# Adapter loads tied to batch 2, the first mask and weight blocks in quarters, and late outputs in halves, in a masked-weight and LoRA kernel

## The chip, the cores and the metric

The kernel runs on one core of a Trainium2 chip. The metric is the device time of one execution in microseconds (us), median over runs. A core has a matrix engine (PE; its weight loads are listed as PEld), a vector engine (DVE), an activation engine (ACT), a GpSimd engine (POOL) and a queue engine (SP) that here only issues transfers. Every engine runs its own instruction stream in order; semaphores make an instruction wait for another engine or for a transfer.

## The reference, cut to what matters

```python
x = x + L0(x, W0, b0, coeff, mask)      # x: 8 x 256 x 1024, mask: 8 x 1024 x 1024 of 0 and 1
x = x + L1(x, itok, W1, b1, lora_A, lora_B)

def L0(h, W, b, coeff, mask):
    sign = 2 * mask - 1                               # +1 or -1
    return einsum('bsi,oi->bso', h, W) + b + einsum('bsi,bio->bso', h, sign) * coeff[:, None, None]

def L1(x, mapping, W, b, lora_As, lora_Bs):           # 32 adapters of rank 16
    h = einsum('bti,bir->btr', x, lora_As[mapping])
    return einsum('bti,oi->bto', x, W) + b + einsum('btr,bro->bto', h, lora_Bs[mapping]) * 2.0
```

All numbers are float32. The mask is 4 MB for each of the eight batches, so that 32 MB of mask have to be read beside 4 MB for each of the two weights and 8 MB of `x`.

## The kernel before, in words

**First layer.** For batch b the effective weight is W0 + I + coeff(b) * (2 mask - 1): `convert` (L401, ACT) turns a loaded block of mask into the signed term in place, and `add` (L314, DVE) adds the block of W0. `w0_sb` stays in SBUF for the whole kernel and the identity (the residual) is added to its diagonal. Batch 0 is multiplied densely (L486): for each of eight chunks c of 128 input rows a mask block `w_0_c` and a W0 chunk are loaded, the first four chunks (`BY_HALF`) in two halves i of the output columns. The tokens `x0_p` come with them, the first one in two halves, on ACT's and SP's queue. Batches 1 to 7 use one level of Strassen-Winograd (`seven`): blocks `w_b_i_g`, sums of blocks s1 to s4 on DVE, sums of tokens t1 to t4 on DVE, and seven products (L657) into PSUM banks X, Y, Z, V. In batch 1 the bank Z first takes s1*t1, ACT reads it out with the bias (`biased`, L569), and the product of s4 is then added to the same bank.

**Second layer.** For each group of four batches, a two-level Winograd product (`product`, L852) with W1. The sums of W1 are computed once in group 0 and kept in DRAM (`keep`, POOL's queue); group 1 loads them again (`left_again`, SP's queue). The adapters are added by `down` (L892, needs all of `la`) and `up` (L923, needs all of `lb`). `lb_pad` holds for each of the four batches 16 rows of lora_B, one row of b1 and zeros; it is cleared by a memset on POOL (L453). `adapters_begin` loads the four rows of b1, `adapters` four pairs of lora_A and lora_B rows at the slot that `itok` names (L809, L812), all on POOL's queue.

**Order.** All work is first recorded as tasks in `Plan`, each with an engine, a duration, reads and writes, and perhaps a due time or `ahead` (it is not planned earlier than so many us ahead of its latest start). `Plan.order` then places the tasks by a list scheduler with fixed costs (`RATE`, `LATENCY`, eight transfers in flight for each kind of queue), and the instructions are emitted in that order. PE's own order is the order of recording. A transfer counts on one of eight semaphores (counters 0 to 7 of SP and ACT together, in turn), so a ninth transfer waits until the one eight places ahead of it has landed. At the end of the program SP waits for these eight counters one after another, 0 first and 7 last.

**Places that the change touches.** The load loop of batch 0 (L421 to L435); the memset of `lb_pad` (L449 to L457); `due` of the two first outputs of batch 0 on DVE (L515); `adapters_begin` and `adapters`; `store`, `Run.done` and the stores of the block c22 (L1134) in the second layer; the call site (L1146); the two cost constants of `Plan`. In group 1 the last product is cut in pieces (`finish`, L1018) whose results are stored on SP, ACT and SP.

Of the kernel before, what the change touches and what calls it, by code (L numbers as in the profile page):

```python
# [13 lines left out]
P = 128  # L14
OH = 512
CG = 2
# [29 lines left out]
class Task:  # L46
    __slots__ = (
        "engine", "n", "busy", "tail", "emit", "before", "after", "bufs", "due", "ls", "ahead",
        "open", "ready", "done", "bytes", "end",
    )  # L50


class Plan:
# [4 lines left out]


    WAKE = 0.07  # L60
    RATE = 400e3
    LATENCY = {"SP": 1.5, "ACT": 1.5, "POOL": 2.5}
    LANES = 8
    MARGIN = 0.3
    TIGHT = 1.0
# [7 lines left out]
    def task(self, engine, busy, tail, emit, reads=(), writes=(), due=None, ahead=None, nbytes=0):  # L73
        k = Task()
        k.engine, k.busy, k.tail, k.emit, k.due, k.ahead = engine, busy, tail, emit, due, ahead
        k.n, k.bytes = len(self.tasks), nbytes
        k.before, k.after = {}, []
        for r in reads:
            for key in r.keys:
                self.need(k, self.writer.get((r.buf, key)))  # L80
        for r in writes:
            for key in r.keys:
                self.need(k, self.writer.get((r.buf, key)))
                for other in self.readers.get((r.buf, key), ()):
                    self.need(k, other)
        for r in reads:
            for key in r.keys:
                self.readers.setdefault((r.buf, key), []).append(k)
        for r in writes:
            for key in r.keys:  # L90
                self.writer[r.buf, key] = k
                self.readers[r.buf, key] = []
        k.bufs = list(dict.fromkeys(r.buf for r in [*writes, *reads]))
        for b in k.bufs:
            b.left += 1
        k.open = len(k.before)
        k.ready = 0.0
        k.done = False
        if engine == "PE":
            k.due = self.pe  # L100
            self.pe += busy
        self.tasks.append(k)
        return k
# [10 lines left out]
    def order(self, slots, idle):  # L114
        for k in reversed(self.tasks):
            late = [a.ls - self.WAKE - self.span(k) for a in k.after]
            if k.engine == "PE":
                late.append(k.due)
            elif k.due is not None:
                late.append(k.due - self.span(k))  # L120
            k.ls = min(late, default=self.pe)
        free = {e: 0.9 for e in ("PE", "DVE", "ACT", "POOL", "SP")}
        places = {kind: [[0.0, i, False] for i in range(n)] for kind, n in slots.items()}
        lanes = {"HW": [0.0] * self.LANES, "SW": [0.0] * self.LANES}
# [110 lines left out]
def kernel(  # L235
# [85 lines left out]
    def dma(engine, o, x, nbytes, due=None, ahead=None, what=None):  # L321
        busy = {"SP": 0.37, "ACT": 0.36, "POOL": 0.53}[engine]
        reads = [x] if isinstance(x, Ref) else []
        writes = [o] if isinstance(o, Ref) else []

        def emit():
            ENGINE[engine].dma_start(  # L327
                o.ap() if isinstance(o, Ref) else o, x.ap() if isinstance(x, Ref) else x
            )

        return plan.task(
            engine, busy, plan.LATENCY[engine], emit, reads, writes, due, ahead, nbytes
        )
# [43 lines left out]
    def x0_ref(p, c=None):  # L377
        return x0[p](ALL if c is None else (c,), (lambda t: t) if c is None else (lambda t: t[:, c]))
# [4 lines left out]
    def part(a, i):  # L383
        flat = a.rearrange("p i f -> (p i f)")
        return flat.rearrange("(i p f) -> i p f", i=2, p=P)[i]
# [25 lines left out]
    def w_part(c, i, o):  # L411
        keys = tuple((i2, q) for i2 in (ALL if i is None else (i,)) for q in halves(o))
        sel = slice(0, 2) if i is None else slice(i, i + 1)
        return w_b0[c](keys, lambda t: t[:, sel, o])
# [5 lines left out]

    every = slice(0, OH)  # L421
    for c in range(NC):
        where = [0, 1] if c < BY_HALF else [None]
        for i in where:
            n = P * OH * 4 * (1 if i is not None else 2)
            w = w_part(c, i, every)
            as_int = w.buf(w.keys, lambda t, f=w.index: f(t).bitcast(I32))
            src = lambda a: part(a, i) if i is not None else a
            sel = lambda r: r if i is None else r.buf(r.keys, lambda t, f=r.index: f(t)[:, 0])
            dma("SP", sel(as_int), src(mask[0, c]), n)  # L430
            dma("SP", sel(w0_part(c, i, every)), src(w0T[c]), n)
            if c == 0:
                dma("ACT" if i == 0 else "SP", x0_ref(0, i), part(x0T[0], i), n // 2)
            elif c % CG == 0 and i in (0, None):
                dma("SP", x0_ref(c // CG), x0T[c // CG], P * CG * T * 4)  # L435

    plan.task(
# [8 lines left out]

    ident_keys = ((0,),)
    plan.task("POOL", 1.2, 0.1, lambda: make_identity(nc, ident.t), (), (ident((0,)),), due=6.0)
    plan.task(  # L449
        "POOL",  # L450
        1.2,
        0.1,
        lambda: nc.gpsimd.memset(lb_pad.t, 0.0),  # L453
        (),
        (lb_pad(tuple(range(2 * GB))),),
        due=30.0,
    )  # L457

    def identity(c):
        h, q = divmod(c * P, OH)  # L460
# [46 lines left out]
    for ot in range(NC):  # L507
        h, j = divmod(ot, TPH)
        ps = dense[ot // 2]((0,), lambda t, k=ot % 2: t[:, k, :])
        o = y[0, h](ALL, lambda t, j=j: t[:, j, :])  # L510
        bias = b0_sb((0,), lambda t, ot=ot: t[:, ot : ot + 1])
        if ot < 2:
            xr = x0_ref(ot // CG, ot % CG)
            dve(
                lambda o=o, ps=ps, bias=bias, xr=xr: nc.vector.scalar_tensor_tensor(  # L515
                    o.ap(), ps.ap(), bias.ap(), xr.ap(), ALU.add, ALU.add
                ),
                T,
                (ps, bias, xr),
                (o,),  # L520
                due=42.0,
            )
        else:
            plan.task(
                "ACT",
                T / 1200 + 0.145,
                0.11,
                lambda o=o, ps=ps, bias=bias: nc.scalar.activation(
                    o.ap(), ps.ap(), AF.Identity, bias=bias.ap()
                ),  # L530
                (ps, bias),
                (o,),
                due=42.0,
            )
# [257 lines left out]
        for u in range(2):  # L792
            add(q[u](ALL), quads[x][u](ALL), quads[z][u](ALL), 1024, op)

    def adapters_begin():
        for i in range(GB):
            row = i * S + R
            dma("POOL", lb_pad((i,), lambda t, r=row: t[r : r + 1, :]), b1, 4096, due=60.0, ahead=25.0)

    def adapters(group):  # L800
        for i in range(GB):
# [20 lines left out]
    def second_layer(group):  # L822
# [53 lines left out]
        def store(o, i, j, u, v, q=None, c=slice(0, CG), tokens=slice(0, T), due=12.0):  # L876
# [6 lines left out]
                due=plan.pe + due,  # L883
            )

        def down():
            ph = bank(f"psh_{group}", 2, T, partial=True)

            def emit():
                for c in range(NC):  # L890
                    for i in range(GB):
                        nc.tensor.matmul(  # L892
                            ph.t[i * S : i * S + R, 0, :],
                            lhsT=la.t[:, i, c, :],
                            rhs=y[GB * group + i, c // TPH].t[:, c % TPH, :],
                            start=c == 0,
                            stop=c == NC - 1,
                        )

            reads = [la((i,)) for i in range(GB)]  # L900
            reads += [y[GB * group + i, h](ALL) for i in range(GB) for h in range(2)]
            pe(32, 3.62, emit, reads, (ph((0,)),))
            for i in range(GB):
                rows = slice(i * S, i * S + R)
                plan.task(
                    "ACT",
                    0.3,
                    0.11,
                    lambda rows=rows: nc.scalar.mul(h_sb.t[rows, :], ph.t[rows, 0, :], SCALING),
                    (ph((0,)),),  # L910
                    (h_sb((i,)),),
                )
# [38 lines left out]
        class Run:  # L951
# [10 lines left out]

            def done(self, *uv):
                if self.dest:
                    store(self.out[uv], *self.dest, *uv)
                if self.then:
                    self.then(uv)

# [161 lines left out]
        for u in range(2):  # L1130
            o2, x2 = (q[u, 0].buf(ALL) for q in (c22, e1))
            add(o2, o2, x2, 1024, due=plan.pe + 5.0)
            for v in range(2):
                store(c22[u, v], 1, 1, u, v)  # L1134
        k.x2()
        k.y()
        k.x3()
# [5 lines left out]

    for group in range(NGROUP):
        for b in range(GB * group, GB * (group + 1)):
            if b == GB * group + 2:  # L1146
                if group == 0:
                    adapters_begin()
                adapters(group)
            if b == 0:  # L1150
                continue
            if b in DENSE:
                dense_batch(b)
            else:
                seven(b)
        second_layer(group)
# [80 lines left out]
```

## Time and profile before

| | |
|---|---|
| median of 3 runs | 402.17 us (402.03 to 403.28) |
| profiled execution: its own time | 401.81 us |
| its span, first to last instruction | 400.1 us |
| PE busy | 394.5 us, 2750 matmuls |
| PEld busy | 360.9 us |
| DVE busy | 326.0 us, 409 instructions |
| ACT busy | 143.3 us |
| POOL busy | 44.4 us |
| moved by transfers | 84.63 MB, mean 211 GB/s |

The span is the time between the first and the last recorded instruction on the core; 1.7 us of the execution's own time lie outside of it. A group's row in the profile gives the line, the engine, the operation, the tile names without numbers, the shape, the busy time and the idle time of the engine ahead of it with what ended that. Big buffers (128 x 1024) all have the name `big`, half ones `small`, PSUM banks `bank`: which product a row is follows from its line and its place in the order.

### The profile page before, as it was taken

What the parts mean: (1) busy time and instruction counts of PE and PEld (TensorE: products, weight loads), DVE (VectorE), ACT (ScalarE), POOL (GpSimd) and SP (SyncE); (2) the same over time, 40 slices, a digit from 0 to 9 for tenths busy, and PEclk for the clock granted to TensorE, in tenths of its full rate; (3) what the DMA queues carried; (4) which work ended last, traced back from release to release, by engine and by line L of the source; (5) the groups of instructions that cost most, each with busy time, mean ns of one, the idle gap of its engine ahead of it and who ended that gap; (6) DMA issues with size and microseconds to landing.
All of it is one profiled execution on the core that took longest, in us unless ns stands there. A gap on an engine that the chain in (4) does not pass through costs nothing.

```text
span 400.1 us, 6933 instructions
## 1 busy us (share of the span) xinstructions
PE 394.5 (99%) x2750; PEld 360.9 (90%) x2750; DVE 326.0 (81%) x409; ACT 143.3 (36%) x249; POOL 44.4 (11%) x87
## 2 busy tenths in 40 slices
PE   8999999999999999999999999999999999999996
PEld 6889999999978888888899999999998888888885
DVE  3548999999999999997999999999737356485574
ACT  5438974712133021017318266472222231100200
POOL 3000400001344241230223000000000000000000
DMA  8999999641477389579679665110101457555934
GB/s 275 400 404 410 367 365 408 218 153 40 172 242 284 113 280 360 196 246 326 242 238 321 207 207 207 61 54 2 26 2 54 114 154 241 177 157 176 290 112 159
DMA packets 30676, 84.63 MB, mean 211 GB/s; under 512 B 4276, under 2 KB 4916, under 8 KB 30644
## 3 DMA queue, kind: packets, MB, share of 16 engines
q1 hardware_dynamic: 24914, 67.19, 49.1%
q0 software_dynamic: 5440, 16.80, 11.2%
q8 instruction: 22, 0.36, 0.4%
q10 hardware_dynamic: 290, 0.20, 0.2%
q14 instruction: 10, 0.08, 0.1%
HBM read 64.25 MB, written 19.92 MB: 210 GB/s over the span
## 4 chain that ended last, share of the span: by engine, by line
PE 83%; DMA 12%; DVE 2%; issue 1%; ACT 1%; SPq 1%
PE bank L852 40%; PE bank L657 39%; DMA big<-mask 9%; DMA w<-w0T 3%; DVE big L314 2%; PE bank L923 2%; PE bank L892 2%; SPq L327 1%; PE bank L1018 0%; ACT big L401 0%; ACT big L569 0%
## 5 line engine op out<-in xcount | busy, mean ns | idle before, releaser
L314 DVE TENSOR_TENSOR big<-big,big 128x1024 f32<-128x1024 f32 (+1 forms) x104 | 116.7, 1138 | 6.7 <-PE bank L657 4.3
L657 PE MATMUL bank<-small,big 128*128 128x128 f32 x896 | 103.6, 275 | 0.3 <-DVE big L314 0.3
L657 PEld LDWEIGHTS bank<-small,big 128*128 128x128 f32 x896 | 101.8, 192 | 0.5 <-DVE big L314 0.5
L314 DVE TENSOR_TENSOR big<-bank,big 128x512 f32<-128x512 f32 (+2 forms) x103 | 68.5, 677 | 38.7 <-PE bank L852 32.1
L852 PE MATMUL bank<-small,small 128*128 128x256 f32 x384 | 89.1, 380 | 0.1
L401 ACT ACTIVATE big<-big,neg_c,two_c 128x1024 f32<-128x1024 int32 (+2 forms) x69 | 79.3, 1182 | 18.7 <-DMA big<-mask 18.3
L314 DVE TENSOR_TENSOR big<-big,w 128x1024 f32<-128x1024 f32 (+2 forms) x69 | 76.8, 1142 | 9.6 <-DMA w<-w0T 5.5
L852 PEld LDWEIGHTS bank<-small,small 128*128 128x128 f32 x384 | 72.7, 190 | 11.1 <-issue 0.8
L657 PE MATMUL bank<-big,big 128*128 128x128 f32 x672 | 78.4, 275 | 0.8 <-ACT big L569 0.8
L657 PEld LDWEIGHTS bank<-big,big 128*128 128x128 f32 x672 | 76.8, 192 | 1.1 <-ACT big L569 1.0
L569 ACT ACTIVATE big<-bank,b 128x128 f32<-128x128 f32 x112 | 32.3, 367 | 73.0 <-PE bank L657 63.5
L852 PE MATMUL bank<-big,small 128*128 128x256 f32 x224 | 52.5, 380 | 0.0
L852 PEld LDWEIGHTS bank<-big,small 128*128 128x128 f32 x224 | 42.3, 190 | 6.3 <-ACT big L318 0.7
L318 ACT COPY bank<-bank 128x512 f32<-128x512 f32 x20 | 11.4, 570 | 85.7 <-PE bank L852 61.8
L318 ACT COPY big<-bank 128x512 f32<-128x512 f32 x32 | 17.6, 593 | 56.7 <-PE bank L852 30.6
L314 DVE TENSOR_TENSOR small<-big,small 128x512 f32<-128x512 f32 x49 | 33.2, 685 | 2.6 <-PE bank L852 2.5
L486 PE MATMUL bank<-small,big 128*128 128x256 f32 x128 | 29.1, 387 | 0.1
L486 PEld LDWEIGHTS bank<-small,big 128*128 128x128 f32 x128 | 24.4, 193 | 4.7 <-DVE big L314 1.0
L852 PE MATMUL bank<-big,big 128*128 128x256 f32 x112 | 26.7, 381 | 0.0
L852 PEld LDWEIGHTS bank<-big,big 128*128 128x128 f32 x112 | 21.0, 190 | 3.4 <-ACT big L318 0.7
L314 DVE TENSOR_TENSOR small<-big,big 128x512 f32<-128x512 f32 x28 | 19.2, 685 | 2.3 <-PE bank L852 2.1
L314 DVE TENSOR_TENSOR small<-big 128x512 f32<-128x512 f32 x28 | 19.2, 684 | 2.1 <-PE bank L852 2.1
(38 smaller groups left out, 122.0 us busy)
## 6 DMA issues: line engine op xcount, KB each, us to landing
big<-mask SPq DMA_DIRECT2D x60, 512.0 KB, 7.2
big<-xT SPq DMA_DIRECT2D x14, 512.0 KB, 5.3
big<-w1T SPq DMA_DIRECT2D x8, 512.0 KB, 4.9
leaf_S_s<-small POOLq DMA_DIRECT2D x16, 256.0 KB, 3.8
outT<-big POOLq DMA_DIRECT2D x16, 256.0 KB, 2.8
small<-leaf_S_s SPq DMA_DIRECT2D x16, 256.0 KB, 3.2
outT<-big SPq DMA_DIRECT2D x15, 256.0 KB, 2.5
leaf_A_s<-small POOLq DMA_DIRECT2D x12, 256.0 KB, 3.0
```

Of the source, the lines that this page charges most:

```text
L314: return dve(lambda: f(o.ap(), x.ap(), y.ap()), n, (x, y), (o,), due)
L318: "ACT", n / 1200 + 0.06, 0.11, lambda: nc.scalar.copy(o.ap(), x.ap()), (x,), (o,), due
L327: ENGINE[engine].dma_start(o.ap() if isinstance(o, Ref) else o, x.ap() if isinstance(x, Ref) else x)
L401: lambda: nc.scalar.activation(o.ap(), x.ap(), AF.Identity, bias=neg_c.t[:, b : b + 1], scale=two_c.t[:, b : b + 1]),
L486: nc.tensor.matmul(dense[ot // 2].t[:, ot % 2, :], lhsT=w_b0[c].t[:, h, j * P : (j + 1) * P], rhs=x0[c // CG].t[:, c % CG, :], start=c == ...
L569: lambda o=o, p=p, bias=bias: nc.scalar.activation(o.ap(), p.ap(), AF.Identity, bias=bias.ap()),
L657: nc.tensor.matmul(ps[:, j, :], lhsT=l[:, c, j * P : (j + 1) * P], rhs=m[:, 2 * a + c, :], start=first and a == 0 and c == 0 and j == 0, s ...
L852: nc.tensor.matmul(ps.t[:, j, :], lhsT=lt[:, c, j * P : (j + 1) * P], rhs=rt[:, c, :], start=start and c == 0 and j == 0, stop=False, skip ...
L892: nc.tensor.matmul(ph.t[i * S : i * S + R, 0, :], lhsT=la.t[:, i, c, :], rhs=y[GB * group + i, c // TPH].t[:, c % TPH, :], start=c == 0, s ...
L923: nc.tensor.matmul(ps[b].t[:, j, :], lhsT=lb_pad.t[rows, o : o + P], rhs=h_sb.t[rows, :], start=j == 0, stop=j == 1, skip_group_check=True,)
```

## The change

The loads of batch 0's first chunk are issued in two quarters and one half (mask and W0 in turn) in place of two halves, and are given the first rank in the planner (`rank`). The memset of `lb_pad` is moved from the start of the program into `adapters_begin`, behind a small ACT copy that reads an element column of batch 2's `y`; a second such copy stands ahead of `la`. `adapters_begin` and `adapters` are recorded one batch later (after batch 2). The rows of b1 lose their due time. The first outputs of batch 0 get the due time 65 in place of 42. Five stores of group 1 (four of c22, one of the last but one block) are issued as two transfers each. `RATE` and `LATENCY` of the planner are changed a little, which moves the order of some other tasks.

```diff
@@ class Plan
-    RATE = 400e3
-    LATENCY = {"SP": 1.5, "ACT": 1.5, "POOL": 2.5}
+    RATE = 396e3
+    LATENCY = {"SP": 1.8, "ACT": 1.8, "POOL": 2.8}
...
-            k.ls = min(late, default=self.pe)
+            k.ls = min(late, default=self.pe) if k.rank is None else k.rank
@@ the loads of batch 0
     for c in range(NC):
-        where = [0, 1] if c < BY_HALF else [None]
-        for i in where:
-            n = P * OH * 4 * (1 if i is not None else 2)
-            w = w_part(c, i, every)
+        where = [(0, every), (1, every)] if c < BY_HALF else [(None, every)]
+        for i, o in parts(0) if c == 0 else where:
+            n = P * (o.stop - o.start) * 4 * (1 if i is not None else 2)
+            w = w_part(c, i, o)
...
-            dma("SP", sel(as_int), src(mask[0, c]), n)
-            dma("SP", sel(w0_part(c, i, every)), src(w0T[c]), n)
-            if c == 0:
-                dma("ACT" if i == 0 else "SP", x0_ref(0, i), part(x0T[0], i), n // 2)
+            for r, a in ((sel(as_int), mask[0, c]), (sel(w0_part(c, i, o)), w0T[c])):
+                dma("SP", r, src(a), n).rank = -1.0 if c == 0 else None
+            if c == 0 and o.stop == OH:
+                dma("ACT" if i == 0 else "SP", x0_ref(0, i), part(x0T[0], i), P * T * 4)
...
-    plan.task(
-        "POOL",
-        1.2,
-        0.1,
-        lambda: nc.gpsimd.memset(lb_pad.t, 0.0),
-        (),
-        (lb_pad(tuple(range(2 * GB))),),
-        due=30.0,
-    )
...
-                due=42.0,
+                due=65.0,
@@ the adapters
-    def adapters_begin():
+    def behind(o, late):
+        plan.task(
+            "ACT",
+            0.2,
+            0.11,
+            lambda: nc.scalar.copy(o.ap(), late.ap().to_broadcast(list(o.ap().shape))),
+            (late,),
+            (o,),
+        )
+
+    def adapters_begin(late):
+        rows = lb_pad(tuple(range(2 * GB)), lambda t: t[:, :1])
+        behind(rows, late)
+        behind(la(tuple(range(GB)), lambda t: t[:, :, 0, 0]), late)
+        plan.task("POOL", 1.0, 0.1, lambda: nc.gpsimd.memset(lb_pad.t, 0.0), (), (rows,))
         for i in range(GB):
             row = i * S + R
-            dma("POOL", lb_pad((i,), lambda t, r=row: t[r : r + 1, :]), b1, 4096, due=60.0, ahead=25.0)
+            dma("POOL", lb_pad((i,), lambda t, r=row: t[r : r + 1, :]), b1, 4096, ahead=25.0)
@@ the second layer
+        def store_halves(o, *where):
+            for half in [slice(c, c + 1) for c in range(CG)] if tail else [slice(0, CG)]:
+                store(o.buf(o.keys, lambda t, f=o.index, h=half: f(t)[:, h]), *where, c=half)
...
-                    store(self.out[uv], *self.dest, *uv)
+                    whole = self.n + 1 < len(OUTER) or uv != (0, 0)
+                    (store if whole else store_halves)(self.out[uv], *self.dest, *uv)
...
-                store(c22[u, v], 1, 1, u, v)
+                store_halves(c22[u, v], 1, 1, u, v)
@@ the call site
-            if b == GB * group + 2:
+            if b == GB * group + 3:
                 if group == 0:
-                    adapters_begin()
+                    adapters_begin(y[2, 0]((0,), lambda t: t[:, 0, :1]))
                 adapters(group)
```

## The prediction

> **What bounds the kernel now.** I read four views in turn: the page's shares and its chain, PE's waits, windows of the stretches with transfers, and the timeline around each wait of PE. First the page's shares, then PE's waits (line, released by: us in total, times, longest):
>
> ```profile
> PE 394.5 (99%) x2750; PEld 360.9 (90%) x2750; DVE 326.0 (81%) x409; ACT 143.3 (36%) x249; POOL 44.4 (11%) x87
> PE bank L348 <- PEq L1226: 0.9, 1, 0.9
> PE bank L657 <- ACT big L569: 0.8, 1, 0.8
> PE bank L657 <- DVE big L314: 0.3, 1, 0.3
> ```
>
> PE is the bound: apart from its start and two waits in batch 1 it hardly pauses. The change adds and removes no matmul, so it can gain only at PE's start, at these two waits and behind PE's end, and lose wherever it makes a new wait. The timeline around both waits (start, length, [idle before <- releaser]):
>
> ```profile
> 45.97 8.04 DVE L314 TENSOR_TENSOR big<-big,big 128x1024 f32<-128x1024 f32 x7
> 47.25 5.62 PE L657 MATMUL bank<-small,big 128*128 128x128 f32 x48 [0.34 <-DVE big L314]
> 48.61 1.12 ACT L569 ACTIVATE big<-bank,b 128x128 f32<-128x128 f32 x4
> 51.36 1.24 ACT L401 ACTIVATE big<-big,neg_c,two_c 128x1024 f32<-128x1024 int32 x1 [1.62 <-DMA big<-mask]
> 52.51 1.12 ACT L569 ACTIVATE big<-bank,b 128x128 f32<-128x128 f32 x4
> 53.68 2.50 PE L657 MATMUL bank<-big,big 128*128 128x128 f32 x20 [0.80 <-ACT big L569]
> ```
>
> Wait 1: PE wants the block sum s1 of batch 1 and DVE ends it at 47.20. PE's matmuls start every 0.11 us in a row; here 0.61 us lie between two starts (46.63 and 47.25), of which the profile calls 0.34 idle. Wait 2: PE may not write bank Z again before ACT has read it (L569, the second row of four). These four reads stand behind a convert (L401) that waited 1.62 us for a mask. The starts of the matmuls around it are 52.60 and 53.68, 1.07 apart. Why the mask was late, by windows (last three numbers: PE's clock, DMA share, GB/s):
>
> ```profile
> 5.00:8.50 3.50, 3.50 (x13) 2.66 (x13) 1.34 (x4) 1.62 (x2) 0.00 (x0) 1.00 0.93 333
> 8.50:20.00 11.50, 11.43 (x54) 9.65 (x52) 6.30 (x11) 5.30 (x6) 0.00 (x0) 1.00 1.05 401
> 40.00:45.30 5.30, 5.30 (x50) 5.30 (x49) 5.27 (x6) 5.30 (x10) 2.25 (x5) 1.00 1.03 410
> 45.30:54.00 8.70, 7.55 (x65) 7.17 (x64) 8.67 (x9) 6.64 (x12) 1.99 (x4) 1.00 1.03 312
> 57.00:113.00 56.00, 56.00 (x495) 55.77 (x494) 55.88 (x69) 21.44 (x45) 5.98 (x11) 1.00 0.58 212
> ```
>
> Up to 45.3 a 512 KB mask lands every 1.28 us. From 45.3 to 54 the transfers are as busy, but move 312 GB/s in place of 410: the adapters' eight loads are on their way there, and six masks take 11.12 us in place of 7.68, which is 3.44 us late. The last two rows I need are of POOL, the issuer of the adapters and of the rows of b1:
>
> ```profile
> L809 POOL DMA_DIRECT2D la<-lora_a x8 | 4.5, 558 | 42.4 <-issue 41.3 <-PE bank L657 1.0
> L327 POOL DMA_DIRECT2D lb<-b x4 | 2.1, 520 | 0.3 <-POOL lb L453 0.3
> ```
>
> **Wait 1.** In the emitted order of the changed kernel the two outputs of batch 0 on DVE (L515, due 65 in place of 42) stand elsewhere. In the order before, both lie between the masks' sums ahead of s1, each worth a step of 0.395 us (36.20 to 36.59). In the order after, one fills a gap in which DVE sat idle for 0.74 us ahead of 35.06 and PE had its bank ready from 34.0; the other stays ahead of s1. So s1 is ready 0.395 us earlier, at 46.80, and PE goes on at 46.85: −0.40. Bounds 0 (something else of DVE's fills it) and −0.61 (all of it).
>
> **Wait 2.** In the emitted order the four reads of Z now stand ahead of the converts of masks `w_2_1_1` and `w_2_1_3`. Their data are there at about 49 to 50 (the row of 48.61 is the same kind of read, unhindered); PE wants the bank at 52.3 or earlier by the gain of wait 1. The margin is 2 us, so it goes whole: −1.07, even if the mask were as late as before. With the adapters gone from this stretch the masks are 3.44 us earlier besides. What is late next: the same kind of read of bank X, which lies behind the convert in the new order at about 52.6 to 53.7 and is wanted at 55.9. It holds.
>
> **The tail.** The last matmul starts at 396.58, DVE's last add (L314) ends at 397.18, the last store is issued on SP at 397.21 and has landed at 398.77. Then SP passes eight waits, one for each counter, that begin at 398.798, .862, .924, .983, 399.044, .104, .165 and .224. The last store is on counter 0, so all eight steps come behind it. In the changed program five stores more have been issued, and the last one is on counter 7: seven steps of 0.061 are done while it flies, −0.43. The five extra issues are 0.33 us each on SP and ACT (the outT row: 0.33 to 0.35), in a queue that waits for PE's results all the time; the one load among them that moves later, of a leaf, at 385.9 in place of 385.3, lands about 3 us after that and is read at 394.9. Nothing.
>
> **The front.** Up to 20.3 PE waits for transfers only: its starts follow the landings of x0 and W0, last `w0_4`, landed at 18.60 and passed to PE at 20.30; from there to 46.6 it does not wait. So this part moves PE by what `w0_4` moves. Gain: the four rows of b1 (16 KB) and adapters are out of it. They were issued from 2.6 to 4.7, and from 5.0 to 8.5 the rate was 333 GB/s. Against the 401 of the next window 3.5 us carry 238 KB less, which is 0.6 us. Loss: two transfers more of SP's queue ahead of `w0_4`, a step of 0.47 us each at 0.86 to 4.14, 0.95 us if the issues set the pace. From 4.8 on each issue waits for a landing eight places ahead (0.37 to 1.3 apart), so most of that is covered. I take −0.30, bounds −0.60 and +0.95; it is the term that I know least. A rule of the Trainium skill speaks against the quarters: "DMA: Bandwidth & Descriptors", section "Anatomy of one DMA — SWDGE (gpsimd) path", has about 2.0 us fixed plus bytes at 436 GB/s for each transfer, and two more in series would be +4.0 by that (an estimate). The trace does not show such a series: in its first 20 us halves of 256 KB land 0.65 to 0.68 apart, blocks of 512 KB 1.28 apart, in proportion to their bytes.
>
> **Adapters, later.** Memset, four rows of b1 and eight loads now wait for `y` of batch 2, written at 75.5 to 77.75, by two small ACT copies behind a convert that ends at 78.88; ACT idles from there to 86.14, so the copies hold up nobody. On POOL: memset 0.95, eight loads in 5.9 us (41.58 to 47.5), so from about 80 to 87 and landed 6.2 us later, about 93. `down` (L892) wants `la` at 114.5, `up` (L923) wants `lb` at 126.9, each 1.8 earlier now. POOL's other work, the stores of W1's leaves, waits for DVE there (23.5 us of idling in front of `leaf_S_s` alone), is not read before 304, and is delayed by 1.9 us by b1's rows: nothing. The loads of W1 that share the transfers with the adapters are read 12 us later or more. The memset beside DVE costs DVE between nothing and 0.95; at PE 0 to 0.13, since DVE leads by 0.8 there (below); I take 0.
>
> **Sum.** 401.81 − 0.40 − 1.07 − 0.43 − 0.30 = 399.61. The profiled execution is 0.36 below the median of 402.17, so the median comes out at 399.97: 400.0. A measurement of this kernel can tell about 0.3%, 1.2 us; faster means below 400.97.
>
> **Rivals.** *DVE becomes the bound.* PE starts earlier by 1.47 behind wait 2 and DVE by 0.40 only; DVE is busy 55.88 of 56 us up to 113. Its lead at the points where PE takes its results was 1.87 at 66.3, 1.92 at 68.1 and 1.89 at 107.4; 0.8 is left of each. If something takes that too, wait 2's gain comes back as a wait there: 400.0 + 1.07 = 401.1, no change. For it: no slack on DVE for 56 us. Against: the leads, and earlier masks. 0.10.
>
> *The issues at the front set the pace:* 400.0 + 1.25 = 401.2, no change. Against it the waits of SP's issues for landings from 4.1 on. 0.06.
>
> *The adapters come too late.* If POOL's issuing starves while DVE is busy, the loads leave only in DVE's first pause, at 113: the memset and eight issues take 6.9 us, the landing 6.2, so the last is there at 126.1 where `down` wants `la` at 112.6. PE's order is fixed, so it stands for 13.5 us: 413.5, slower. It decides from a last landing of `la` later than 112.6. "SBUF — State Buffer", section "SBUF: two separate sides", describes such starving of POOL's descriptors by DVE's two-port operations. Against it, from 41 to 48 DVE was busy for 6.93 of 7.00 us and the eight issues took 0.49 to 0.57 each. 0.05.
>
> *The change doesn't do what it says:* the last store lands on another counter in time, or an earlier one lands last: 400.0 + 0.43 = 400.4, in the range and faster all the same. 0.03.
>
> **Numbers.** The forecast itself has 0.76. Its low end: 0.30 more at the front and 0.21 more at wait 1 give 399.5, less 0.1 for the spread of the runs, 399.3. The high end takes in the first two rivals (401.1, 401.2) with 0.13 for the memset: 401.3. Faster by over 0.3%: 0.79; within 0.3%: 0.16; slower: 0.05.
>
> **What would show it.** After: PE's waits without the L569 and the L314 row; from 45.3 to 54 near 410 GB/s; `la` issued near 81 and landed by 95; the four reads of Z near 49 to 50; PE past 20.3 by 0.3 earlier; one short step, not eight, behind the last landing. Wrong: a new PE wait between 54 and 127, a front that is later than 20.3, or L809 issues that are stretched.

## The result and the profile after

| | before | after |
|---|---|---|
| median | 402.2 us (401.34 to 405.77, 17 runs) | 401.2 us (400.71 to 402.04, 17 runs) |
| profiled execution: own time, span | 401.81, 400.1 us | 400.71, 399.0 us |
| PE starts its last matmul at | 396.58 us | 395.90 us |
| from there to the end of the span | 3.57 us | 3.14 us |

The ratio is 0.997, with a 95% interval of 0.9958 to 0.9982. The kernel is faster by 0.3%, half of what was forecast (400.0), and inside the range (399.3 to 401.3), near its upper end. PE's waits after (line, released by: us in total, times, longest):

```profile
PE bank L477 <- DVE big L314: 1.1, 1, 1.1
PE bank L348 <- PEq L1236: 0.9, 1, 0.9
```

Both waits of batch 1 (the old L657 rows) are gone. In their place stands one in the dense batch (L477 is the old L486), longer than either: from 7.4 to 8.9, for the second half of the first blocks. The 17th matmul of batch 0 starts at 10.70 in place of 9.67, and this one microsecond is kept up to the matmuls of `w0_4`. The windows, in the order from and to, five engines, clock, DMA share and GB/s:

```profile
2.00:5.00 3.00, 2.93 (x10) 2.48 (x10) 0.67 (x3) 2.37 (x4) 0.00 (x0) 1.00 0.73 228
5.00:8.50 3.50, 2.75 (x9) 1.94 (x8) 1.00 (x3) 0.81 (x1) 0.00 (x0) 1.00 0.88 313
8.50:20.00 11.50, 11.13 (x52) 9.78 (x53) 5.64 (x11) 6.12 (x7) 0.00 (x0) 1.00 1.05 398
45.30:54.00 8.70, 8.70 (x81) 8.70 (x80) 8.67 (x8) 8.70 (x15) 0.00 (x0) 1.00 1.02 408
```

The last row is what was hoped for: 408 GB/s in place of 312, and PE busy all 8.70 us. The first row is of a stretch that the prediction left out: for the kernel before it reads

```profile
2.00:5.00 3.00, 2.92 (x9) 2.34 (x8) 0.55 (x3) 2.38 (x4) 2.38 (x5) 1.00 1.09 318
```

The transfer engines were full there before (share 1.09), and are idle for a quarter of the time after (0.73). The first two windows together moved 228 x 3.0 + 313 x 3.5 = 1780 KB in place of 318 x 3.0 + 333 x 3.5 = 2120 KB; the 340 KB that are missing are 0.85 us at 400 GB/s. The chain of the first 60 us after, by start and length:

```profile
0.86 0.38 SPq L327
...
1.30 0.42 SPq L327
...
2.71 0.43 SPq L327
...
3.19 4.74 DMA w<-w0T
...
7.94 5.06 DMA small<-x0T
...
13.02 6.60 DMA w<-w0T
...
20.04 1.24 DVE big L314
...
21.32 14.08 PE bank L477 x64
```

It begins with five of SP's issues, one every 0.47 us, and then hands over from landing to landing (each issue waits for the counter of the transfer eight places ahead) until `w0_4`, which landed at 19.62 in place of 18.60. PE goes on behind it at 21.32 in place of 20.30. The issues alone are not the difference: the chain of the kernel before begins with the same five at the same times, and goes on with

```profile
3.19 5.23 DMA w<-w0T
```

What differs is what they carry. The six transfers that SP has issued by then are six halves of 256 KB before, 1.5 MB, and four quarters and two halves after, 1.0 MB. The second half of W0's first chunk, for which PE waits, is issued at 3.19 in place of 2.24 and lands at 7.92 in place of 6.73.

The timeline around batch 1's old waits:

```profile
45.73 7.53 PE L648 MATMUL bank<-small,big 128*128 128x128 f32 x66
46.20 8.04 DVE L314 TENSOR_TENSOR big<-big,big 128x1024 f32<-128x1024 f32 x7
49.42 1.44 ACT L560 ACTIVATE big<-bank,b 128x128 f32<-128x128 f32 x5
50.74 2.38 ACT L401 ACTIVATE big<-big,neg_c,two_c 128x1024 f32<-128x1024 int32 x2
53.10 1.17 PE L648 MATMUL bank<-big,big 128*128 128x128 f32 x9
```

The reads of Z (four of the five of L560) end at 50.87, ahead of the converts, and PE starts the second product into Z at 53.10 without a gap. The adapters, from POOL's timeline:

```profile
78.33 0.95 POOL L800 MEMSET lb<- 128x1024 f32 x1 [76.91 <-ACT lb L791]
79.87 0.68 POOL L814 DMA_DIRECT2D la<-lora_a  x1 [0.58 <-issue]
80.54 0.51 POOL L817 DMA_DIRECT2D lb<-lora_b  x1
...
85.83 0.51 POOL L817 DMA_DIRECT2D lb<-lora_b  x1
```

They leave within 6.5 us; the rows of b1 follow at 98.3. `down` starts at 113.82 without a wait.

From the matmul starts the difference adds up: +1.02 behind `w0_4`, −0.61 for wait 1, −1.07 for wait 2, −0.42 for the tail: −1.08 of the −1.10 measured.

### The profile page after: what moved, and what is told of

Its sections match the earlier page's. It is cut to its first block, busy times and chain, and to the rows that moved or that the text cites. A ratio compares the mean times of both kernels' runs of the same rounds, so it can differ in the third digit from the quotient of the medians.

```text
span 399.0 us, 6942 instructions
## 1 busy us (share of the span) xinstructions
PE 393.9 (99%) x2750; PEld 361.0 (90%) x2750; DVE 325.2 (82%) x409; ACT 142.8 (36%) x251; POOL 44.5 (11%) x87
## 4 chain that ended last, share of the span: by engine, by line
PE 91%; DMA 4%; DVE 2%; issue 1%; SPq 1%; DVEq 0%
PE bank L648 44%; PE bank L857 40%; PE bank L477 4%; DMA w<-w0T 3%; DVE big L314 2%; PE bank L932 2%; PE bank L901 2%; DMA small<-x0T 1%; SPq L327 1%; PE bank L1028 0%; DVE w L314 0%; DVEq L314 0%
## 5 line engine op out<-in xcount | busy, mean ns | idle before, releaser
L314 DVE TENSOR_TENSOR big<-big,big 128x1024 f32<-128x1024 f32 (+1 forms) x104 | 116.7, 1140 | 6.8 <-PE bank L648 4.4
L314 DVE TENSOR_TENSOR big<-bank,big 128x512 f32<-128x512 f32 (+2 forms) x103 | 68.6, 678 | 37.2 <-PE bank L857 30.8
L314 DVE TENSOR_TENSOR big<-big,w 128x1024 f32<-128x1024 f32 (+2 forms) x69 | 77.1, 1145 | 10.1 <-ACT big L401 5.0
L560 ACT ACTIVATE big<-bank,b 128x128 f32<-128x128 f32 x112 | 32.2, 369 | 72.6 <-PE bank L648 56.0
L314 DVE TENSOR_TENSOR small<-big,small 128x512 f32<-128x512 f32 x49 | 33.6, 687 | 5.7 <-PE bank L857 5.6
L477 PE MATMUL bank<-small,big 128*128 128x256 f32 x128 | 29.2, 389 | 1.2 <-DVE big L314 1.1
L477 PEld LDWEIGHTS bank<-small,big 128*128 128x128 f32 x128 | 24.8, 196 | 5.5 <-DVE big L314 2.0
L314 DVE TENSOR_TENSOR small<-big 128x512 f32<-128x512 f32 x28 | 19.2, 687 | 1.5 <-PE bank L857 1.5
L314 DVE TENSOR_TENSOR small<-big,big 128x512 f32<-128x512 f32 x28 | 19.3, 688 | 1.1 <-PE bank L857 1.1
```

The lines of the kernel that those rows point to most:

```text
L314: return dve(lambda: f(o.ap(), x.ap(), y.ap()), n, (x, y), (o,), due)
L477: nc.tensor.matmul(dense[ot // 2].t[:, ot % 2, :], lhsT=w_b0[c].t[:, h, j * P : (j + 1) * P], rhs=x0[c // CG].t[:, c % CG, :], start=c == ...
L560: lambda o=o, p=p, bias=bias: nc.scalar.activation(o.ap(), p.ap(), AF.Identity, bias=bias.ap()),
```

## The experiments

The theory after the result: the quarters at the front cost 1.02 us, because SP's issues stand 0.47 us apart at the start whether they carry a quarter or a half; 128 KB in that time are about 276 GB/s, 256 KB about 550. What else could be: the late front only took the place of other waits; it comes from something else (the rank, b1's rows); each transfer has a price of its own.

**The quarters undone (e1).**

```diff
-        for i, o in parts(0) if c == 0 else where:
+        for i, o in where:
```

> The kernel after, with the first block of mask and W0 loaded in halves again (the rank stays). Theory: the quarters starved the transfers, because SP needs 0.47 us for an issue and a quarter carries only 128 KB, and PE's place behind w0_4 (20.30 before, 21.32 after) was late by that for the rest of the run. Then PE starts behind w0_4 at 20.0 to 20.3, the execution is shorter by 1.0 than the kernel after, less 0.12 since the last store is now on counter 5 and not 7, and less some 0.2 of a wait for s1 that comes back: about 399.9 in the profiled execution, 400.4 as a median, ratio to before 0.9945 to 0.9965. Rival 1, the late front only took the place of the waits in batch 1: PE is early at 20.3 but waits 0.8 to 1.0 between 45 and 54, and the time is that of the kernel after plus 0.1. Rival 2, the front is late for something else (rank, or b1 and the memset gone): 21.3 stays.

Measured: 400.36 us (399.95 to 400.92, 10 runs), ratio 0.9948 (0.993 to 0.9967); 0.84 below the kernel after. Its profile was taken of the longest of these runs, 400.92: there `w0_4` landed at 19.06 and PE went on behind it at 20.75, with 301 GB/s from 5 to 8.5. The first window is mended:

```profile
2.00:5.00 3.00, 2.92 (x9) 2.35 (x8) 0.44 (x3) 2.37 (x4) 0.00 (x0) 1.00 0.97 322
```

PE's wait for s1 came back (0.57 between two starts, 0.3 idle by the profile), the one for ACT did not. In this execution the wait took up all that PE had gained at `w0_4`, 0.57: its last matmul starts at 395.89, in the kernel after at 395.90. That is rival 1, in the slowest of the ten runs. The median speaks against it as the rule, and so do the later profiles with halves in the new order (e2, e7, e9, e10), whose last matmul starts 0.48 to 0.95 earlier than that of the kernel after. The window shows that the loss came from the quarters and not from the rank, which stayed (rival 2). PE's place, 20.75, was outside of the 20.0 to 20.3 expected because `w0_4` landed late: PE waited there, and went on 1.70 behind the landing as in the kernels before and after. Why it landed at 19.06 in this execution, later than in any other profile with halves, is not known.

**The rows of b1 early again (e2).** In addition to e1 the memset and the four rows move from `adapters_begin` back to the start of the program:

```diff
...
+    plan.task("POOL", 1.2, 0.1, lambda: nc.gpsimd.memset(lb_pad.t, 0.0), (), (lb_pad(tuple(range(2 * GB))),), due=30.0)
+    for i in range(GB):
+        row = i * S + R
+        dma("POOL", lb_pad((i,), lambda t, r=row: t[r : r + 1, :]), b1, 4096, due=60.0, ahead=25.0)
```

> As the run before it, and in addition the memset of lb and the four rows of b1 stand at the start of the program again, as in the kernel before; the eight adapter loads stay behind batch 2. It prices b1's rows alone. The prediction's term: PE starts behind w0_4 0.3 later than in the run with halves and late rows (bounds 0 to 0.6). Rival: 16 KB in rows of 4 KB, issued by POOL, cost nothing at the front: the same place of PE within 0.1, and the same time.

Measured: 400.52 us (400.08 to 401.19, 12 runs), ratio 0.9956 (0.994 to 0.9971), no different from e1. `w0_4` landed at 18.44, earlier than in e1. Over the profiles with halves it landed at 18.44 to 18.77 with b1's rows at the front (before, e2, e4, e8) and at 18.29 to 19.06 without (e1, e3, e7, e9, e10); the means are both 18.59. The rows cost nothing that can be seen in these profiles or in the time, and the 333 GB/s from 5 to 8.5 was no work of theirs.

**The adapters' part alone (e3).** The kernel before, with the memset, b1's rows and the adapters' loads as in the change; nothing else.

> The kernel before with the adapters' part alone: memset, rows of b1 and eight loads behind batch 2. The emitted order of ACT and DVE around 46 to 54 is that of before: the reads of Z stand behind the convert of mask w_2_1_1. Theory: the mask lands at about 47.9 in place of 51.33, the convert ends by 49.2, the reads by 50.2, and PE's wait for ACT is gone; the wait for s1 stays at 0.6. Profiled execution 401.81 - 1.07, and up to 0.3 less at the front: 400.45 to 400.75. Rival, only the order of ACT matters: the wait for ACT stays at 0.8 or more, 401.5 to 401.8.

Measured: 400.89 us (400.65 to 401.76, 12 runs), ratio 0.9967 (0.9951 to 0.9983), profiled 400.93. The timeline:

```profile
47.10 5.62 PE L647 MATMUL bank<-small,big 128*128 128x128 f32 x48 [0.34 <-DVE big L314]
49.26 1.29 ACT L401 ACTIVATE big<-big,neg_c,two_c 128x1024 f32<-128x1024 int32 x1
50.40 1.19 ACT L559 ACTIVATE big<-bank,b 128x128 f32<-128x128 f32 x4
52.56 1.61 PE L647 MATMUL bank<-big,big 128*128 128x128 f32 x13
```

The order on ACT is the old one, the reads still stand behind the convert, and PE does not wait: the mask is early enough. It landed at 49.05, though, and not at 47.9; the 3.44 us were the delay at the end of the six transfers (four masks and two loads of `x`), and this mask is the third of them. The profiled 400.93 is above the 400.45 to 400.75 expected: at 124.0, with PE now 1.22 earlier than before, it waited 0.24 for a sum of DVE (L314), which the kernel before, the kernel after and e7 do not show.

**The order alone (e4).**

```diff
-    RATE = 400e3
-    LATENCY = {"SP": 1.5, "ACT": 1.5, "POOL": 2.5}
+    RATE = 396e3
+    LATENCY = {"SP": 1.8, "ACT": 1.8, "POOL": 2.8}
...
-                due=42.0,
+                due=65.0,
```

> The kernel before with the planner's two constants and the due time 65 alone: transfers as before, so the mask w_2_1_1 lands at 51.3 again, but the four reads of Z stand ahead of its convert, and one of the two L515 of DVE stands in the earlier gap. Theory: PE's wait for ACT is gone though the mask is late, and the wait for s1 falls from 0.61 to about 0.2: 401.81 - 1.07 - 0.40 = 400.35. Rival, the late masks come back as another wait of PE between 54 and 60: 400.9 to 401.4.

Measured: 401.09 us (400.52 to 401.83, 12 runs), ratio 0.9968 (0.9952 to 0.9984), profiled 400.72. The reads stand ahead, and the late mask (landed 51.43) holds up only its own convert:

```profile
49.07 1.14 ACT L569 ACTIVATE big<-bank,b 128x128 f32<-128x128 f32 x4 [0.31 <-PE bank L657]
51.45 1.24 ACT L401 ACTIVATE big<-big,neg_c,two_c 128x1024 f32<-128x1024 int32 x1 [1.24 <-DMA big<-mask]
52.45 1.73 PE L657 MATMUL bank<-big,big 128*128 128x128 f32 x14
```

So wait 2 has two cures, and the change applies both; together they gain no more than one. The time was a miss: 400.35 was expected, and the median is in the rival's range. The rival is there in small: at 55.9 two starts of PE lie 0.26 apart and the next two 0.21, together 0.25 us over the usual step, for reads of ACT (L569) that stand behind the next late convert. The wait for s1 shrank to 0.19 between two starts.

**W0's quarters issued by ACT (e5).**

```diff
-            for r, a in ((sel(as_int), mask[0, c]), (sel(w0_part(c, i, o)), w0T[c])):
-                dma("SP", r, src(a), n).rank = -1.0 if c == 0 else None
+            for q, r, a in (("SP", sel(as_int), mask[0, c]),
+                            ("ACT" if o != every else "SP", sel(w0_part(c, i, o)), w0T[c])):
+                dma(q, r, src(a), n).rank = -1.0 if c == 0 else None
```

> The kernel after, with the same quarters, but the two quarters of W0 are issued by ACT in place of SP, side by side with those of mask; what is loaded and in what pieces stays. Theory (SP's issue step of 0.47 us starves the transfers while each issue carries 128 KB): the two issues are off SP's queue, w0_4 lands at 18.4 to 19.1 as with halves and not at 19.6, PE starts behind it at 20.2 to 20.8 and not at 21.3, time 400.2 to 400.6. PE's very start is later by about 0.5, since ACT's other issues and its first convert move back, which the wait for w0_4 hides. Rival (a transfer has a price of its own, whoever issues it): w0_4 stays at 19.6, PE at 21.3, 401.2 or more.

Measured: 401.86 us (401.17 to 403.06, 12 runs), ratio 0.9988 (0.9978 to 0.9997): a miss in the time. Its first windows moved 277 x 3.0 + 358 x 3.5 = 2080 KB, nearly what the kernel before did, and `w0_4` landed at 19.16 and not at 19.6; that is about half of the way back to the 18.59 of the halves. So much is the theory's; whether the rest is a price of each transfer or comes from the other loads on ACT's queue is open. The time was lost elsewhere. The load of the coefficients went behind the two issues on ACT's queue:

```profile
PE bank L361 <- DMA c_row<-coeff: 2.5, 1, 2.5
```

With it the first convert and PE's real start moved back, from 4.95 to 7.41. I had put that at 0.5 us, hidden. PE then ran without a pause and reached the matmuls of `w0_4` at 21.99, 0.67 later than in the kernel after. At its last matmul 0.21 of that was left, and the last store of this execution landed 2.10 us after its issue in place of 1.58; the profiled 401.46 is made of these, the median 0.4 above it is not explained.

**All of the first block in quarters (e6).**

```diff
-        for i, o in parts(0) if c == 0 else where:
+        for i, o in [(0, slice(0, OQ)), (0, slice(OQ, OH)), (1, slice(0, OQ)), (1, slice(OQ, OH))] if c == 0 else where:
```

> The kernel after, with the second half of the first block in quarters too: two issues more on SP, the suspected cost doubled. Theory: w0_4 lands 0.95 later than in the kernel after, at 20.5, PE starts behind it at 22.2, and the end is later by as much, plus 0.37 for a last store that is now on counter 1: 401.2 + 0.95 + 0.37 = 402.5. Rival (the late front is no matter of issues): w0_4 at 19.6, 401.5.

Measured: `w0_4` landed at 20.50 and PE went on behind it at 22.20, both as worked out. The chain shows SP's issues one behind the other for much longer, up to 7.46, before a landing sets the pace:

```profile
6.51 0.43 SPq L327
...
6.98 0.43 SPq L327
...
7.46 5.74 DMA w<-w0T
```

Time 402.1 us (401.5 to 402.43, 12 runs), ratio 0.9989 (0.9977 to 1.0001); its profiled execution, also 402.10, is 1.39 above that of the kernel after where 1.32 was expected, but the median, 0.9 above, is less than the 402.5 forecast. Two transfers more cost 0.88 us at `w0_4`, close to two issues, 0.95. The Trainium skill ("DMA: Bandwidth & Descriptors", "Anatomy of one DMA — SWDGE (gpsimd) path") has 2.0 us fixed for each transfer, measured on transfers that GpSimd issues. By that two more in series would cost 4.0, an estimate; the trace, of transfers that SP issues, does not agree with adding it up so.

**Halves, the order and the counter together (e7, and e9 once more).** The kernel after without its quarters; `due` 36 places DVE's two outputs of batch 0 where the kernel after has them, and two more stores in halves put the last store on counter 7 again:

```diff
-        for i, o in parts(0) if c == 0 else where:
+        for i, o in where:
...
-                due=65.0,
+                due=36.0,
...
-                    whole = self.n + 1 < len(OUTER) or uv != (0, 0)
+                    whole = (self.n, uv) not in ((4, (0, 0)), (4, (0, 1)), (6, (0, 0)))
```

> The kernel after without its quarters, with due 36 in place of 65 (DVE's two L515 then stand where the kernel after has them) and two stores of c12 in halves, which puts the last store on counter 7 again. Meant to keep both gains of the change without its loss. Theory: e1's 400.36 less 0.12 for the counter, less 0.1 to 0.2 as s1 is ready 0.3 earlier and PE then waits for itself only: 400.1, ratio 0.994 to 0.996. Rival: s1 was no longer what PE waits for, and the two more stores cost issue time: 400.3 to 400.5.

> The kernel of e7 again, beside the next two on the same chip: 400.0 to 400.4. In nearly all its profiles PE's first matmuls take 0.427 us a step and switch to 0.216 at some point between 6.4 and 9.0 us, another one in each execution; the theory is that this is now the front, since PE no longer waits for w0_4.

Measured: 400.32 us (399.68 to 401.29, 6 runs), ratio 0.9949 (0.9934 to 0.9965), and 400.21 us (399.71 to 400.38, 6 runs), ratio 0.9947 (0.993 to 0.9965). It beats the kernel before by 0.5% and the kernel after by 0.9 us; over e1 the gain is too small to tell. In e7's profile PE runs from its start to the end of batch 1 (all of its waits, then the chain up to 60 us):

```profile
PE bank L348 <- PEq L1236: 0.9, 1, 0.9
```

```profile
2.74 2.43 PE bank L348 x6
5.17 29.28 PE bank L477 x128
34.45 25.57 PE bank L648 x229
```

No transfer and no other engine is on it. Not every execution is like this: in e9's profile `w0_4` landed at 18.76 in place of 18.48, PE waited for it, and two starts at s1 lie 0.37 apart; its last matmul starts 0.45 later than e7's.

**The late halves alone (e8).** The kernel before with `store_halves` at its five places.

> The kernel before with the late stores in halves alone; the last store is then on counter 5. Theory: five steps of 0.061 pass while it flies, the end is 0.30 sooner: 401.5 in the profiled execution if its front is that of the kernel before, last issue to SP's drain 1.78 in place of 2.08, all before the last matmul unchanged. Rival (the earlier halves are late themselves, and the wait for them takes the place of the steps): 2.0 or more from the last issue to the drain.

Measured: 1.78 from the last issue (397.746) to SP's drain (399.527), as expected. In the total it does not show: 402.13 us (401.42 to 404.45, 12 runs), ratio 1.0003 (0.9987 to 1.0019); 0.30 us is below what the runs can tell. Its profiled execution, 402.04, had a wait 2 of 1.4 and not 1.0.

**PE busy from the start (e10, e11).** The kernel of e7 and the kernel after, each with

```diff
-    idle(T)
+    idle(T, T // 4)
```

> The kernel of e7 with one more idle matmul (64 columns) between the first one and that of the coefficients, so that PE has no gap of 0.3 us at 1.9 to 2.2. Theory: the switch to the full rate needs a stretch of some 3.4 us in which PE was busy all along, and the gap breaks it; then the switch comes by up to 1.7 us sooner, between 4.4 and 7.7, PE reaches the matmuls of w0_4 as soon as that has landed, at 20.0 to 20.3, and the median is 0.2 lower than that of e7's kernel. Rival: so small a gap is of no account, the switch stays between 6.1 and 9.5, and so does the time.

> The kernel after with the same idle matmul. By the theory that its front is set by the landing of w0_4 (19.6, PE behind it at 21.3), the half rate is hidden there and the time stays at 400.7 to 401.3, whether or not the switch comes sooner. Rival: if the half rate mattered in the kernel after too, it gains as much as e7's kernel does, or loses as little.

Measured: 400.18 us (399.9 to 400.37, 6 runs), ratio 0.995 (0.9934 to 0.9967), and 400.94 us (400.51 to 401.79, 11 runs), ratio 0.9972 (0.996 to 0.9983): no difference from the kernels without the extra matmul. The half rate ended at 7.9 in e10 and at 5.6 in e11, the former outside of what the theory allowed; what sets the moment stays open. In e11 PE still stood at `w0_4` until 21.48, so a sooner full rate was of no use there.

## Why the prediction was right or wrong

**The front failed.** The step was "From 4.8 on each issue waits for a landing eight places ahead [...], so most of that is covered". It was true of the stretch from 4.8 on and looked past the one ahead of it: from 0.9 to 5.1 the issues set the pace, 0.47 us apart, and four of them carried half as much; the bytes that were missing then were never made up for, since the transfers ran at 400 GB/s afterwards. The term −0.30 measured +1.02; its upper bound, 0.95, was nearly the value, and the rival built on it (0.06) gave 401.2, the median. Of the 1.10 us by which the profiled execution missed the sum (400.71 for 399.61) 1.32 are the front's, and 0.21 came back at wait 1. The range held because its upper end was drawn to take in that rival; the forecast itself failed here. The gain in the term was nothing either: the low rate from 5 to 8.5 was put down to b1's rows because they were there at the time (e2).

**Wait 1: right in mechanism, overtaken.** In the new order DVE ends s1 0.43 earlier than before when counted from the transfers ahead of it, at 0.395 worked out. But these landed 0.66 later (`x_1_0` at 36.98 in place of 36.32), so s1 was ready at 47.43, not at 46.80. The whole 0.61 went, and not 0.40, because PE came 1.02 later itself: luck, paid for by the front.

**Wait 2: right,** −1.07 as forecast. The margin that was named (reads at 49 to 50, wanted at 52.3) was 50.87 and 53.1. That "even if the mask were as late as before" it would go is what e4 shows; that the earlier masks alone would do is e3, at 2.28 us earlier and not 3.44.

**The tail: right.** 2.08 us from the last issue to SP's drain before, 1.66 after, −0.42 at −0.43 forecast; 1.78 on counter 5 (e8).

**The adapters: right.** They left POOL from 79.9 to 86.3 beside a DVE that was busy for 17.93 of the 18 us from 78 to 96, and neither they nor the moved memset made a wait.

**The sum of the rest.** e7, the change without its quarters and with another `due`, starts its last matmul 1.63 earlier than before, where waits 1 and 2 and the front were put at 1.77. The parts are not those of the forecast: −0.63 at wait 1, −1.07 at wait 2, and +0.07 at `w0_4`.

**The rivals.** DVE did not become the bound: behind 54 no wait of PE came up that the kernel before did not have. The 0.24 at 124.0 in e3 is this rival in small, though. The late adapters, and so the slower case, did not happen.

## What to carry to other kernels

At the start of a kernel, where the queues are still empty, what counted here is bytes per issue: divide a transfer's bytes by the issue step and compare with the rate that the transfer engines reach later; below it, smaller pieces start the first engine sooner and everything else later. Look at the DMA share of the first few microseconds on its own, since an average over ten hides it. When a wait has two causes, try each alone before counting a gain for both.

## What the runs showed of the hardware

PE's first matmuls go at half the later rate, one start every 0.427 us in place of 0.216, and the moment at which that changes differs from one execution to the next: 6.2 us in e8's profile, 6.7 in the kernel after's, 7.8 in e7's, 8.7 in e2's, though PE had much the same work in all. Each microsecond of it costs PE half of one. A kernel that waits for `w0_4` hides that, as the kernels before and after do. In the profiles of e2, e4, e7 and e10 PE did not wait at `w0_4` but came to it 0.3 to 0.6 us later than 1.70 behind its landing; there PE's own work, the half rate included, set the front. The clock column of the windows reads 1.00 all the same. The Trainium skill ("TensorE: Matmul & The Clock Gate", "Part 1: The HAM clock gate") has the matrix engine at half its clock until a free-running window of about 3.4 us was busy, so that the number of slow matmuls varies from run to run. The traces agree on the two rates and on the variation (the change comes between batch 0's 2nd and 9th matmul), with a wider spread, 2.5 us, than the 0.5 us to either side that the page gives.
